# Scores stage of a graph attention kernel: engine order held to source order, outer sums placed one by one between bank reads, adjacency loads two steps ahead

## The chip, the cores and the metric

The kernel runs on one core of one Trainium2 chip. The metric is the device time of that core in microseconds, the median of several executions; lower is better. The profile is one execution taken by the hardware profiler, so its span differs slightly from the median.

A core has a matrix engine (TensorE), a vector engine (VectorE, "DVE" in the profile), an activation engine (ScalarE, "ACT"), GpSimd ("POOL") and a queue engine (SyncE, "SP"). In this kernel SyncE issues nearly all loads, and GpSimd issues the stores. The program is written with a framework that records instructions in source order, works out their dependencies, and then lets a scheduler choose the order in which each engine gets its own instructions. All data are 32-bit floats.

## What is computed

The reference has two layers on a graph of 3327 nodes with 512 features. Cut to what matters:

```python
# layer 0
h = maximum(layernorm(x), 0)
q = h @ Wq.T + bq ; k = h @ Wk.T + bk ; v = h @ Wv.T + bv
a = q @ k.T / sqrt(512) + adj + adj
x = x + softmax(a) @ v
# layer 1
h = maximum(layernorm(x), 0)
A2 = adj + eye
d = diagonal(A2) ** -0.5
temp = A2 @ h @ W.T
x = x + relu((d[:, None] * A2 * d[None, :]) @ temp)
```

The kernel multiplies large matrices in seven half-size products in place of eight (a Winograd form of Strassen's scheme), so sums and differences of blocks are formed on VectorE. The **scores stage** computes exp(2 adj + q k) for 52 steps: four groups (two strips of columns, each in two halves) of 13 row pairs. Each step multiplies a pair of row tiles of the transposed scores with 448 columns (groups 1 and 2) or 384 columns (groups 3 and 4). In the same step it forms the four block sums of A2 that layer 1 will need ("outer sums") from the adjacency blocks that are in SBUF anyway, and stores them.

## The kernel before: the parts that matter

The rings of buffers and the slots that the projection stage (the stage before) uses:

```python
    def ring(*slots):
        turn = itertools.cycle(slots)
        def take(shape, name):
            kind, k = next(turn)
            return kind(k, shape, name)
        return take

    def four_differences(b):
        nc.vector.tensor_sub(b[4], b[0], b[1])
        nc.vector.tensor_add(b[5], b[3], b[4])
        nc.vector.tensor_sub(b[6], b[1], b[3])
        nc.vector.tensor_sub(b[7], b[2], b[5])

    # ... (cut)
    x_bank, y_bank, z_bank, tp_bank = psum_ring(0, 1), psum_ring(2, 3), psum_ring(4, 5), psum_ring(6, 7)

    class Chain:                       # seven products of one step, in three PSUM banks
        before = None
        def __init__(self, product, first, more, last):
            X, Y, Z = x_bank("X"), y_bank("Y"), z_bank("Z")
            product(Y, "m1", True)
            first(0, Y, -1)
            product(Z, "p5", True)
            first(3, Z, -1)
            product(X, "p2", True)
            more(0, X)
            product(Y, "p6", False)
            first(1, Y, -1)
            Chain.finish()             # the last product of the step before
            product(Z, "p3", False)
            more(1, Z)
            product(Y, "p7", False)
            more(3, Y)
            def rest():
                product(Y, "p4", False)
                first(2, Y, 1)
                last()
            Chain.before = rest
        # ... finish() calls Chain.before (cut)

    x_ring = ring(*((mid, k) for k in range(4)))
    v_ring = ring(*((mid, k) for k in range(5, 13)))
```

The scores stage:

```python
    groups = [(s, q) for s in range(2) for q in range(2)]
    g_rings = ring(*((mid, k) for k in range(4))), ring(*((mid, k) for k in range(4, 9)))
    o_ring = ring(*((mid, k) for k in range(9, 13)))
    # ... queries(n) loads four query blocks of group n (cut)

    def more_queries(n, qt):
        # ... (cut)
        four_differences(qt)
        nc.scalar.mul(qt[0], qt[0], -1.0)

    def adjacency(s, q, t):                                  # two loads of a step
        wd, c = Q[s], q * Q[s]
        g = [take([P, 2, Q[0]], f"g{k}")[:, :, :wd] for k, take in enumerate(g_rings)]
        for k in range(2):
            # ... (cut)
            nc.sync.dma_start(g[k], src[:, :, c : c + wd])   # L416
        return g

    def outer_sums(s, q, t, g):
        wd, c = Q[s], q * Q[s]
        pair = [o_ring([P, 2, Q[0]], "o")[:, :, :wd] for _ in range(2)]
        o = [pair[m // 2][:, m % 2] for m in range(4)]
        nc.vector.tensor_add(o[0], g[0][:, 0], g[0][:, 1])   # L423
        nc.vector.tensor_add(o[1], g[1][:, 1], g[0][:, 1])
        nc.vector.tensor_add(o[2], o[1], g[0][:, 0])
        nc.vector.tensor_add(o[3], o[2], g[1][:, 0])
        for n, parts in enumerate(((0, 2, 3), (0, 1, 2, 3), (3,), (1, 2, 3))):
            k, y = divmod(n, 2)
            d = diagonal(o[0], (k * HALF + t) * P, STRIPS[s] * P + y * H[s] + c)
            for m in parts if d else ():
                nc.vector.tensor_add(o[m][:, d[0]], o[m][:, d[0]], d[1])      # L431, + identity
        for m in range(2):
            nc.gpsimd.dma_start(sumd[s][t][:, 2 * m : 2 * m + 2, c : c + wd], pair[m])   # L433

    def scores(s, q, t, qt, g):
        # ... (cut)
        def product(ps, name, start):
            for k in range(2):
                nc.tensor.matmul(ps[:, :wd], h_of(t, name, k), qt[B[name]][:, k], ...)   # L441

        def settle(k):
            # ... (cut)
            nc.scalar.activation(g[k], g[k], AF.Exp)                                     # L448
            nc.gpsimd.dma_start(pd[s][t][:, 2 * k : 2 * k + 2, c : c + wd], g[k])        # L449

        def first(n, ps, sign):                                                          # L452
            nc.vector.scalar_tensor_tensor(a[n], a[n], 2.0, ps[:, :wd], op0=ALU.mult,
                                           op1=ALU.add if sign > 0 else ALU.subtract)

        def more(n, ps):
            nc.vector.tensor_add(a[n], a[n], ps[:, :wd])                                 # L456
            if n == 1:
                settle(0)

        Chain(product, first, more, lambda: settle(1))

    steps = [(n, t) for n in range(len(groups)) for t in range(HALF)]
    coming = queries(0)
    more_queries(0, coming)
    ahead = [adjacency(*groups[n], t) for n, t in steps[:1]]
    for k, (n, t) in enumerate(steps):
        if t == 0:
            qt = coming
        if k + 1 < len(steps):
            ahead.append(adjacency(*groups[steps[k + 1][0]], steps[k + 1][1]))
        g = ahead.pop(0)
        outer_sums(*groups[n], t, g)
        scores(*groups[n], t, qt, g)
        if n + 1 < len(groups):
            if t == 4:
                coming = queries(n + 1)
            if t == 8:
                more_queries(n + 1, coming)
    Chain.finish()
```

A 32-bit matmul of the source becomes two in the trace, so one product (two source matmuls) is four matmuls there, and a step has 28.

Of the kernel before, what the change touches and what calls it, by code (L numbers as in the profile page):

```python
# [3 lines left out]

# [40 lines left out]
def graph_layers_kernel(  # L45
# [27 lines left out]
    nc = tc.nc  # L73
# [28 lines left out]
    def half(k, shape, name):  # L102
        return arena.tile(shape, F32, name=name, tag=f"half{k}")
# [7 lines left out]
# [7 lines that stand above are left out]

        return take

    const = ctx.enter_context(tc.tile_pool(name="const", bufs=1))
    dram = ctx.enter_context(tc.tile_pool(name="dram", bufs=1, space=bass.MemoryType.DRAM))
    small = ctx.enter_context(tc.tile_pool(name="small", bufs=4))
# [24 lines left out]
    sumd = [[dram.tile([P, len(SUMS), H[s]], F32, name=f"sum{s}_{t}") for t in range(HALF)] for s in range(2)]  # L148
# [9 lines left out]

    def four_differences(b):

        nc.vector.tensor_sub(b[4], b[0], b[1])
        nc.vector.tensor_add(b[5], b[3], b[4])
        nc.vector.tensor_sub(b[6], b[1], b[3])  # L163
        nc.vector.tensor_sub(b[7], b[2], b[5])

    def diagonal(a, r0, c0):


        lo, hi = max(r0, c0), min(r0 + P, c0 + a.shape[-1])
        return (slice(lo - c0, hi - c0), ident[:, lo - r0 : hi - r0]) if lo < hi else None  # L170
# [24 lines left out]
    def h_of(t, product, c):  # L195

        k = next(k for k, (a, n) in enumerate(PACKS) if a <= t < a + n)
        o = (t - PACKS[k][0]) * P
        return hp[k][:, A[product], c, o : o + P]
# [7 lines left out]
    class Chain:  # L207
# [5 lines left out]
        before = None  # L213
# [29 lines left out]
                Chain.before()  # L243
            Chain.before = None

    x_ring = ring(*((mid, k) for k in range(4)))
    v_ring = ring(*((mid, k) for k in range(5, 13)))

    def load_x(i, queue=nc.sync):
        xt = x_ring([P, D], "xt")  # L250
# [35 lines left out]
                             start=c == 0, stop=c == DC - 1)  # L286
    nc.vector.tensor_scalar(u, pu[:, :DC], scale, None, op0=ALU.mult)
    for b in (M, w_v):
        four_differences(b)
        nc.scalar.mul(b[0], b[0], -1.0)  # L290

    def h_transposed(k):
# [93 lines left out]
    groups = [(s, q) for s in range(2) for q in range(2)]  # L386
# [4 lines left out]
    def queries(n):  # L391

        s, q = groups[n]
        wd = Q[s]
        qt = [half(k, [P, 2, Q[0]], "qt")[:, :, :wd] for k in q_slots[n % 2][:4]]
        for k in range(2):
            for y in range(2):
                c = STRIPS[s] * P + y * H[s] + q * wd
                nc.sync.dma_start(qt[2 * k + y], qd[:, 2 * k : 2 * k + 2, c : c + wd])
        return qt  # L400

    def more_queries(n, qt):

        wd = Q[groups[n][0]]
        qt += [half(k, [P, 2, Q[0]], "qt")[:, :, :wd] for k in q_slots[n % 2][4:]]
        four_differences(qt)
        nc.scalar.mul(qt[0], qt[0], -1.0)

    def adjacency(s, q, t):

# [3 lines that stand above are left out]
            r0, c0 = (k * HALF + t) * P, STRIPS[s] * P  # L414
            src = adjT[r0 : r0 + P, c0 : c0 + 2 * H[s]].rearrange("p (y w) -> p y w", y=2)
            nc.sync.dma_start(g[k], src[:, :, c : c + wd])  # L416
        return g

    def outer_sums(s, q, t, g):
        wd, c = Q[s], q * Q[s]  # L420
        pair = [o_ring([P, 2, Q[0]], "o")[:, :, :wd] for _ in range(2)]
        o = [pair[m // 2][:, m % 2] for m in range(4)]
        nc.vector.tensor_add(o[0], g[0][:, 0], g[0][:, 1])  # L423
        nc.vector.tensor_add(o[1], g[1][:, 1], g[0][:, 1])  # L424
        nc.vector.tensor_add(o[2], o[1], g[0][:, 0])
        nc.vector.tensor_add(o[3], o[2], g[1][:, 0])
        for n, parts in enumerate(((0, 2, 3), (0, 1, 2, 3), (3,), (1, 2, 3))):
            k, y = divmod(n, 2)
            d = diagonal(o[0], (k * HALF + t) * P, STRIPS[s] * P + y * H[s] + c)
            for m in parts if d else ():  # L430
                nc.vector.tensor_add(o[m][:, d[0]], o[m][:, d[0]], d[1])  # L431
        for m in range(2):
            nc.gpsimd.dma_start(sumd[s][t][:, 2 * m : 2 * m + 2, c : c + wd], pair[m])  # L433

    def scores(s, q, t, qt, g):
        wd, c = Q[s], q * Q[s]
        a = [g[0][:, 0], g[0][:, 1], g[1][:, 0], g[1][:, 1]]

        def product(ps, name, start):
            for k in range(2):  # L440
                nc.tensor.matmul(ps[:, :wd], h_of(t, name, k), qt[B[name]][:, k], start=start and k == 0, stop=k == 1,  # L441
                                 skip_group_check=True)

        def settle(k):
            if k == 1 and t == HALF - 1:
                nc.scalar.activation(g[k], g[k], AF.Exp, bias=pad)
            else:
                nc.scalar.activation(g[k], g[k], AF.Exp)  # L448
            nc.gpsimd.dma_start(pd[s][t][:, 2 * k : 2 * k + 2, c : c + wd], g[k])  # L449

        def first(n, ps, sign):
            nc.vector.scalar_tensor_tensor(a[n], a[n], 2.0, ps[:, :wd], op0=ALU.mult,  # L452
                                           op1=ALU.add if sign > 0 else ALU.subtract)

        def more(n, ps):
            nc.vector.tensor_add(a[n], a[n], ps[:, :wd])  # L456
            if n == 1:
                settle(0)

        Chain(product, first, more, lambda: settle(1))  # L460

    steps = [(n, t) for n in range(len(groups)) for t in range(HALF)]
    coming = queries(0)
    more_queries(0, coming)
    ahead = [adjacency(*groups[n], t) for n, t in steps[:1]]
    for k, (n, t) in enumerate(steps):
        if t == 0:
            qt = coming
        if k + 1 < len(steps):
            ahead.append(adjacency(*groups[steps[k + 1][0]], steps[k + 1][1]))  # L470
        g = ahead.pop(0)
        outer_sums(*groups[n], t, g)
        scores(*groups[n], t, qt, g)
        if n + 1 < len(groups):
            if t == 4:
                coming = queries(n + 1)
            if t == 8:
                more_queries(n + 1, coming)
    Chain.finish()


    ROLE = {"p1": 0, "p6": 2, "p7": 4, "p5": 6, "p2": 7, "p3": 1, "p4": 5, "p8": 3}
# [30 lines left out]
    for s in range(2):  # L513
        for k0 in range(0, HT[s], 2):
            n = min(2, HT[s] - k0)
            units += [(s, k0, n, t) for t in range(HALF)]
    pts, fresh = {}, {}

    def fetch(k):
        if k < len(units):  # L520
            if k < HALF:
                fresh[k] = values(units[k][3])
            pts[k] = weights(*units[k])
# [50 lines left out]
    for k, (s, k0, n, t) in enumerate(units):  # L574
        fetch(k + 3)
        if k < HALF:
            four_differences(fresh.pop(k))
        pt = pts.pop(k)
        o = o_ring2([P, 4, 2 * P], "o")[:, :, : n * P]
        four_sums(o, pt)  # L580
        if t == 0:
            ps = seven()
            sums = sum_ring([P, 2, 2 * P], "sums")[:, :, : n * P]
            nc.vector.tensor_add(sums, pt[:, 0:2], pt[:, 2:4])
        else:
            nc.vector.tensor_add(sums, sums, pt[:, 0:2])  # L586
            nc.vector.tensor_add(sums, sums, pt[:, 2:4])
        for r, a, b in (
            ("p1", pt[:, 0], 0), ("p6", o[:, 2], 4), ("p7", o[:, 0], 5), ("p5", o[:, 1], 3),
            ("p2", pt[:, 2], 1), ("p3", o[:, 3], 2), ("p4", pt[:, 3], 6),  # L590
        ):
            for m in range(n):
                nc.tensor.matmul(ps[r][:, m * E : (m + 1) * E], a[:, m * P : (m + 1) * P], vr[t][:, b],  # L593
                                 start=t == 0 and m == 0, stop=t == HALF - 1, skip_group_check=True)
        if t == HALF - 1:
            attend(s, k0, n, sums, ps)
# [48 lines left out]
    parts = {}  # L645
# [50 lines left out]
    class Right:  # L696
# [31 lines left out]
        def make(self):  # L728
            own, r = self.own, self.r
            if r == "p5":  # L730
                nc.vector.tensor_sub(own, self.two[:, :, 0:E], self.two[:, :, E:D])  # L731
            if r == "p6":
                nc.vector.tensor_add(own, own, self.two[:, :, 0:E])
                nc.vector.tensor_sub(own, own, self.two[:, :, E:D])
                nc.gpsimd.dma_start(self.t2[:, 0 : 2 * self.n], self.b[:, 0 : 2 * self.n])
            if r in ("p7", "p4"):
                nc.vector.tensor_sub(own, own, self.one)
            if self.n == 2:
                four_differences([self.b[:, k] for k in range(8)])

    class Step:

# [106 lines left out]
    steps = [Step(g, r, s, t, rights[g, r, t]) for g in range(2) for r in ORDER for s in range(2) for t in every]  # L849
# [10 lines left out]
    for g in range(2):  # L860
        for n, r in enumerate(ORDER):
            for t, e in enumerate(every):
                k = number_of(g, n, 0, t)
# [427 lines left out]
```

## Time and profile before

| | |
|---|---|
| time, median of 3 runs | 2365.53 us (2365.27 to 2374.09) |
| span of the profiled execution | 2365.2 us |
| busy: TensorE / VectorE / ScalarE / GpSimd | 2256.0 / 1420.9 / 227.7 / 294.6 us |
| scores stage: first and last matmul start | 205.6 and 815.9 us |
| matmuls of the scores stage (L441) | 1456, that is 28 in each of 52 steps |
| an adjacency load, issue to landing | 4.1 us median (3.2 to 6.5) |
| a store of exponentials / of outer sums, issue to landing | 3.8 / 4.8 us (448 columns) |

How to read the lines that follow. A line of a list of waits has the engine and source line that waited, what it waited for, then the total in us, how often, and the longest. "PEld" is the weight load of TensorE, "SPq" the sequencer of the load queue. A timeline line has the start and the busy time in us, the engine, the line, the operation, output<-input, how many were merged, and in brackets the idle time of that engine just before and what ended it. A table of stretches gives the stretch and its length, then the busy time of each engine with its number of instructions, the granted TensorE clock as a share of full speed, the mean busy share of the 16 DMA engines, and GB/s. The profile models the ends of matmuls, so the spacing of their starts says more than their durations.

### The profile page before, as it was taken

The numbers are of one execution on the slowest core, as the hardware profiler recorded it, in microseconds if no ns is written. First come the engines' busy times: TensorE is split into PE (matmuls) and PEld (weight loads), VectorE is DVE, ScalarE is ACT, GpSimd is POOL, SyncE is SP. The second block draws the span as 40 slices with busy tenths as digits, with TensorE's granted clock in tenths as the row PEclk, the third lists the DMA queues.
The fourth block names the chain that finished last, engine by engine and source line by source line (L and its number), as shares of the span: only waits on it lengthen the run. The fifth ranks groups of instructions, "written<-read, shape, count | busy, mean of one in ns | idle before, by whom it ended". The sixth has DMA issues, their size and how long they took to land.

```text
span 2365.2 us, 22424 instructions
## 1 busy us (share of the span) xinstructions
PE 2256.0 (95%) x7522; PEld 1413.1 (60%) x7522; DVE 1420.9 (60%) x2935; ACT 227.7 (10%) x322; POOL 294.6 (12%) x462
## 2 busy tenths in 40 slices
PE   7999898988888899999999999999999999999996
PEld 4765444444544588888888755555555455555554
DVE  5436556555565556557556676777744456777674
ACT  4221111111111100000000000000000000000011
POOL 2323222222222101101011100000000000000001
PEclk8999999999999999999999999999999999999998
DMA  4336767766667634426346577766655567767684
GB/s 144 132 116 233 241 231 250 238 216 226 210 238 260 205 95 147 134 77 190 89 135 223 177 230 246 232 201 194 204 170 167 177 193 240 229 209 221 200 276 142
DMA packets 230412, 457.62 MB, mean 193 GB/s; under 512 B 25394, under 2 KB 135696, under 8 KB 230288
## 3 DMA queue, kind: packets, MB, share of 16 engines
q1 hardware_dynamic: 192464, 322.12, 44.1%
q0 software_dynamic: 37248, 132.93, 15.3%
q8 instruction: 61, 1.00, 0.2%
q10 hardware_dynamic: 576, 1.05, 0.1%
q14 instruction: 63, 0.52, 0.1%
HBM read 323.11 MB, written 132.90 MB: 193 GB/s over the span
## 4 chain that ended last, share of the span: by engine, by line
PE 59%; issue 28%; POOL 6%; DMA 4%; DVE 2%; ACT 0%; POOLq 0%; SPq 0%; DVEq 0%; ACTq 0%
PE p L768 27%; PE p L593 17%; PE p L827 4%; POOL sum L433 3%; PE p L760 2%; POOL p L449 2%; PE Y L352 2%; PE Y L321 2%; PE Z L352 1%; PE Z L321 1%; DMA p<-g 1%; DMA g<-in_adjT_dram 1%; PE mm L277 1%; POOL out_dram L88 1%; PE tp L301 0%
## 5 line engine op out<-in xcount | busy, mean ns | idle before, releaser
L768 PE MATMUL p<-part,b 128*128 128x448 f32 (+1 forms) x2352 | 835.4, 513 | 2.4 <-DVE b L731 1.6
L768 PEld LDWEIGHTS p<-part,b 128*128 128x128 f32 x2352 | 445.4, 190 | 374.1 <-issue 210.0
L441 PE MATMUL Y<-qt,hp 128*128 128x448 f32 (+1 forms) x832 | 330.9, 539 | 68.6 <-DVE g L452 68.3
L593 PE MATMUL p<-vr,o 128*128 128x256 f32 x1352 | 323.2, 380 | 3.4 <-DVE vr L163 2.2
L441 PEld LDWEIGHTS Y<-qt,hp 128*128 128x128 f32 x832 | 160.2, 197 | 220.9 <-DVE g L452 93.5
L593 PEld LDWEIGHTS p<-vr,o 128*128 128x128 f32 x1352 | 257.2, 190 | 40.0 <-DVE vr L163 2.6
L155 DVE TENSOR_TENSOR part<-part 128x896 f32<-128x896 f32 (+1 forms) x168 | 171.9, 1024 | 164.4 <-PE p L768 104.9
L593 PE MATMUL p<-vr,pt 128*128 128x256 f32 x1014 | 250.8, 380 | 0.0
L593 PEld LDWEIGHTS p<-vr,pt 128*128 128x128 f32 x1014 | 192.7, 191 | 26.6
L441 PE MATMUL Z<-qt,hp 128*128 128x448 f32 (+1 forms) x416 | 166.3, 523 | 0.0
L586 DVE TENSOR_TENSOR sums<-sums,pt 128x512 f32<-128x512 f32 (+1 forms) x84 | 54.8, 652 | 139.4 <-DMA pt<-p 139.4
L448 ACT ACTIVATE g<-g 128x896 f32<-128x896 f32 (+1 forms) x100 | 89.6, 896 | 467.5 <-DVE g L452 327.2
L452 DVE SCALAR_TENSOR_TENSOR g<-g,Y 128x448 f32<-128x448 f32 (+1 forms) x156 | 91.2, 585 | 64.0 <-PE Y L441 62.9
L423 DVE TENSOR_TENSOR o<-g 128x448 f32<-128x448 f32 (+1 forms) x52 | 30.8, 592 | 163.8 <-DMA g<-in_adjT_dram 159.2
L441 PEld LDWEIGHTS Z<-qt,hp 128*128 128x128 f32 x416 | 81.9, 197 | 70.0 <-issue 44.7
L449 POOL DMA_DIRECT2D p<-g x104 | 75.4, 725 | 290.1 <-ACT g L448 272.1
L433 POOL DMA_DIRECT2D sum<-o x104 | 75.4, 726 | 170.4 <-DVE o L424 123.7
L157 DVE TENSOR_TENSOR part<-part,part 128x384 f32<-128x384 f32 (+1 forms) x146 | 86.1, 590 | 8.9 <-DVE part L156 0.5
L156 DVE TENSOR_TENSOR part<-part,part 128x384 f32<-128x384 f32 (+1 forms) x146 | 86.1, 590 | 3.1
L760 PE MATMUL p<-part,b 128*128 128x448 f32 (+1 forms) x224 | 82.8, 513 | 0.0
L441 PE MATMUL X<-qt,hp 128*128 128x448 f32 (+1 forms) x208 | 81.1, 513 | 0.0
L566 POOL DMA_DIRECT2D x1d<-xt x26 | 14.5, 558 | 456.2 <-DVE xt L565 445.8
(174 smaller groups left out, 1924.0 us busy)
## 6 DMA issues: line engine op xcount, KB each, us to landing
part<-sum SPq DMA_DIRECT2D x104, 448.0 KB, 4.7
pt<-p SPq DMA_DIRECT2D x78, 512.0 KB, 4.1
part<-sum SPq DMA_DIRECT2D x104, 384.0 KB, 3.5
part<-in_adjT_dram SPq DMA_DIRECT2D x78, 448.0 KB, 4.3
part<-in_adjT_dram SPq DMA_DIRECT2D x78, 384.0 KB, 3.6
g<-in_adjT_dram SPq DMA_DIRECT2D x52, 448.0 KB, 4.2
sum<-o POOLq DMA_DIRECT2D x52, 448.0 KB, 4.8
p<-g POOLq DMA_DIRECT2D x52, 448.0 KB, 3.8
```

The lines of the kernel that those rows point to most:

```text
L155: nc.vector.tensor_add(o[:, 0:2], g[:, 0:4:3], g[:, 1:2].to_broadcast([P, 2, g.shape[-1]]))
L156: nc.vector.tensor_add(o[:, 2], o[:, 1], g[:, 0])
L157: nc.vector.tensor_add(o[:, 3], o[:, 2], g[:, 2])
L433: nc.gpsimd.dma_start(sumd[s][t][:, 2 * m : 2 * m + 2, c : c + wd], pair[m])
L441: nc.tensor.matmul(ps[:, :wd], h_of(t, name, k), qt[B[name]][:, k], start=start and k == 0, stop=k == 1, skip_group_check=True)
L448: nc.scalar.activation(g[k], g[k], AF.Exp)
L449: nc.gpsimd.dma_start(pd[s][t][:, 2 * k : 2 * k + 2, c : c + wd], g[k])
L452: nc.vector.scalar_tensor_tensor(a[n], a[n], 2.0, ps[:, :wd], op0=ALU.mult, op1=ALU.add if sign > 0 else ALU.subtract)
L593: nc.tensor.matmul(ps[r][:, m * E : (m + 1) * E], a[:, m * P : (m + 1) * P], vr[t][:, b], start=t == 0 and m == 0, stop=t == HALF - 1, ski ...
L760: nc.tensor.matmul(ps[("p2", "p3", "p4", "p8")[k]][:, :w], b[:, z], a[:, 0, y], start=k == 3, stop=True)
L768: nc.tensor.matmul(ps[r][:, :w], b[:, i], m, start=self.t == 0, stop=self.t == PAIRS - 1 and r in ("p1", "p5", "p6", "p7"))
L827: nc.tensor.matmul(ps, cts[s][y][d][:, k * P : (k + 1) * P], w1[d], start=d == 0, stop=d == DC - 1)
```

## The change

Three things are done, all for the scores stage. A context manager `in_order` adds a dependency without a semaphore from each instruction of VectorE, TensorE, GpSimd and SyncE in the stage's loop to the one before it on the same engine, so that the scheduler must keep the source's order among them (ScalarE is left free, and so are instructions of other stages). The outer sums become a generator: the sums for step k+1 are given out one by one, each after a bank read of step k; the pieces on the diagonal follow in twos, and the query differences of the next group one in a step. Adjacency is loaded two steps ahead in the source where it was one. With this the slots of the projection stage's x and V buffers are changed, so that the first adjacency blocks and sums find their slots free earlier. The computation is the same.

```diff
+    @contextmanager
+    def in_order(*engines):
+        traced = nc.cur_bb.bb.instructions
+        before = traced[-1]
+        yield
+        begin = next(k for k in reversed(range(len(traced))) if traced[k] is before) + 1
+        last = {}
+        for ins in traced[begin:]:
+            if ins.engine in engines:
+                if ins.engine in last:
+                    tc.add_manual_dep(ins, last[ins.engine].name, ...NoSync...)
+                last[ins.engine] = ins
@@ four_differences: each of the four operations is now yielded
-        nc.vector.tensor_sub(b[4], b[0], b[1])
+        yield nc.vector.tensor_sub(b[4], b[0], b[1])
 ... (cut: the other three likewise; other stages run the generator to its end at once)
-    x_ring = ring(*((mid, k) for k in range(4)))
-    v_ring = ring(*((mid, k) for k in range(5, 13)))
+    x_ring = ring(*((mid, k) for k in (0, 1, 2, 5)))
+    v_ring = ring(*((mid, k) for k in (9, 10, 11, 12, 3, 6, 7, 8)))
@@ more_queries
-        four_differences(qt)
+        for _ in four_differences(qt):
+            yield
         nc.scalar.mul(qt[0], qt[0], -1.0)
+        yield
@@ outer_sums
-        nc.vector.tensor_add(o[0], g[0][:, 0], g[0][:, 1])
-        nc.vector.tensor_add(o[1], g[1][:, 1], g[0][:, 1])
-        nc.vector.tensor_add(o[2], o[1], g[0][:, 0])
-        nc.vector.tensor_add(o[3], o[2], g[1][:, 0])
+        of = ((g[0][:, 0], g[0][:, 1]), (g[1][:, 1], g[0][:, 1]), (o[1], g[0][:, 0]), (o[2], g[1][:, 0]))
+        crossing = []
 ... (cut: the diagonal's marks are collected in crossing)
+        for m in range(4):
+            nc.vector.tensor_add(o[m], *of[m])
+            yield
+            if m % 2 and not crossing:
+                nc.gpsimd.dma_start(sumd[s][t][:, m - 1 : m + 1, c : c + wd], pair[m // 2])
+        for k, (m, d) in enumerate(sorted(crossing, key=lambda mark: mark[0])):
+            nc.vector.tensor_add(o[m][:, d[0]], o[m][:, d[0]], d[1])
+            if k % 2:
+                yield
-        for m in range(2):
+        for m in range(2) if crossing else ():
             nc.gpsimd.dma_start(sumd[s][t][:, 2 * m : 2 * m + 2, c : c + wd], pair[m])
@@ scores: first(...) and more(...) end with
+            next(beside, None)
@@ the loop
-    more_queries(0, coming)
-    ahead = [adjacency(*groups[n], t) for n, t in steps[:1]]
-    for k, (n, t) in enumerate(steps):
 ... (cut)
+    for _ in more_queries(0, coming):
+        pass
+    ahead = [adjacency(*groups[n], t) for n, t in steps[:2]]
+    for _ in outer_sums(*groups[0], 0, ahead[0]):
+        pass
+    with in_order(*(e.engine for e in (nc.vector, nc.tensor, nc.gpsimd, nc.sync))):
+        for k, (n, t) in enumerate(steps):
+            if t == 0:
+                qt = coming
+            g = ahead.pop(0)
+            if k + 2 < len(steps):
+                ahead.append(adjacency(*groups[steps[k + 2][0]], steps[k + 2][1]))
+            pieces_of = []
+            if k + 1 < len(steps):
+                pieces_of.append(outer_sums(*groups[steps[k + 1][0]], steps[k + 1][1], ahead[0]))
+            if n + 1 < len(groups):
+                if t == 2:
+                    coming = queries(n + 1)
+                    pieces_more = more_queries(n + 1, coming)
+                if t >= 6:
+                    pieces_of.append(itertools.islice(pieces_more, 1))
+            beside = itertools.chain(*pieces_of)
+            scores(*groups[n], t, qt, g)
+            for _ in beside:
+                pass
+        Chain.finish()
```

More of the change, by code (lines that the diff above doesn't have):

```diff
@@ L2 @@
 import math
-from contextlib import ExitStack
+from contextlib import ExitStack, contextmanager
 import concourse.bass as bass
@@ L119, in ring @@
         return take
+    @contextmanager
[8 more added lines that the diff above has]
+                if ins.engine in last:
+                    tc.add_manual_dep(ins, last[ins.engine].name,
+                                      mybir.DependencyInfo(mybir.DependencyClass.NoSync, mybir.DependencyReason.DATA),
+                                      reason="in_order")
+                last[ins.engine] = ins
     const = ctx.enter_context(tc.tile_pool(name="const", bufs=1))
@@ L159, in four_differences @@
     def four_differences(b):
-        nc.vector.tensor_sub(b[4], b[0], b[1])
-        nc.vector.tensor_add(b[5], b[3], b[4])
-        nc.vector.tensor_sub(b[6], b[1], b[3])
-        nc.vector.tensor_sub(b[7], b[2], b[5])
+        yield nc.vector.tensor_sub(b[4], b[0], b[1])
+        yield nc.vector.tensor_add(b[5], b[3], b[4])
+        yield nc.vector.tensor_sub(b[6], b[1], b[3])
+        yield nc.vector.tensor_sub(b[7], b[2], b[5])
     def diagonal(a, r0, c0):
@@ L288, in graph_layers_kernel @@
     for b in (M, w_v):
-        four_differences(b)
+        for _ in four_differences(b):
+            pass
         nc.scalar.mul(b[0], b[0], -1.0)
@@ L429, in outer_sums @@
             d = diagonal(o[0], (k * HALF + t) * P, STRIPS[s] * P + y * H[s] + c)
-            for m in parts if d else ():
-                nc.vector.tensor_add(o[m][:, d[0]], o[m][:, d[0]], d[1])
-        for m in range(2):
+            crossing += [(m, d) for m in parts] if d else []
+        for m in range(4):
[8 more added lines that the diff above has]
+        for m in range(2) if crossing else ():
             nc.gpsimd.dma_start(sumd[s][t][:, 2 * m : 2 * m + 2, c : c + wd], pair[m])
@@ L458, in more @@
                 settle(0)
+            next(beside, None)
         Chain(product, first, more, lambda: settle(1))
@@ L463, in graph_layers_kernel @@
     coming = queries(0)
-    more_queries(0, coming)
-    ahead = [adjacency(*groups[n], t) for n, t in steps[:1]]
-    for k, (n, t) in enumerate(steps):
[L467 to L479, printed above, removed]
+    for _ in more_queries(0, coming):
[22 more added lines that the diff above has]
+            for _ in beside:
+                pass
+        Chain.finish()
     ROLE = {"p1": 0, "p6": 2, "p7": 4, "p5": 6, "p2": 7, "p3": 1, "p4": 5, "p8": 3}
@@ L576, in graph_layers_kernel @@
         if k < HALF:
-            four_differences(fresh.pop(k))
+            for _ in four_differences(fresh.pop(k)):
+                pass
         pt = pts.pop(k)
@@ L738, in make @@
             if self.n == 2:
-                four_differences([self.b[:, k] for k in range(8)])
+                for _ in four_differences([self.b[:, k] for k in range(8)]):
+                    pass
     class Step:
```

## Prediction

> **What bounds the kernel now.** I read the page's busy shares and its 40 slices first. TensorE is busy 95% of the span, so only a stage in which it is not busy can give time back. The slices show full TensorE from about 850 us on; earlier, the scores stage (matmuls of line 441) has 8s and 9s. The listing of line 441 puts its first matmul at 205.6 us and its last at 815.9 us. A table of two stretches inside this stage and one of the attention stage shows the difference:
>
> ```profile
> core 0: us, PE busy (x) PEld busy (x) DVE busy (x) ACT busy (x) POOL busy (x), PEclk, DMA share, GB/s
> 233.00:505.00 272.00, 246.01 (x628) 119.81 (x629) 154.75 (x304) 43.68 (x46) 66.68 (x92) 0.98 0.69 235
> 530.00:780.00 250.00, 221.55 (x636) 125.27 (x635) 137.82 (x287) 38.11 (x45) 65.91 (x91) 0.94 0.69 232
> 900.00:1200.00 300.00, 299.61 (x1401) 263.56 (x1401) 182.39 (x450) 16.78 (x22) 30.55 (x54) 1.00 0.44 137
> ```
>
> In the scores stage no engine is full: TensorE 90% and 89%, VectorE 57% and 55%, DMA 69%. The granted clock is also below 1, while full load in attention runs at 1.00. So waits bind here, not work. The list of waits between 205 and 816 us names them:
>
> ```profile
> DVE o L423 <- DMA g<-in_adjT_dram: 159.2, 46, 6.0
> PEld Y L441 <- DVE g L452: 93.5, 47, 5.0
> PE Y L441 <- DVE g L452: 68.3, 39, 4.4
> ...
> SPq L416 <- DMA p<-g: 479.6, 95, 14.1
> ```
>
> TensorE waits for VectorE's read of a Y bank (L452). But VectorE idles itself, 159.2 us in 46 of 52 steps, always ahead of L423, the first outer sum of A2, and for an adjacency load. The load queue (last line, from the waits of the queue itself) in turn waits 479.6 us for stores of exponentials. The timeline of VectorE and TensorE from 612 us shows one turn:
>
> ```profile
> 612.20 0.56 DVE L452 SCALAR_TENSOR_TENSOR g<-g,Y 128x384 f32<-128x384 f32 x1 [0.74 <-PE Y L441]
> 617.28 0.56 DVE L423 TENSOR_TENSOR o<-g 128x384 f32<-128x384 f32 x1 [4.53 <-DMA g<-in_adjT_dram]
> 617.75 0.55 DVE L452 SCALAR_TENSOR_TENSOR g<-g,Y 128x384 f32<-128x384 f32 x1
> ...
> 610.70 2.74 PE L441 MATMUL Y<-qt,hp 128*128 128x384 f32 x8
> 613.28 1.45 PE L441 MATMUL Z<-qt,hp 128*128 128x384 f32 x4
> 614.57 1.45 PE L441 MATMUL Y<-qt,hp 128*128 128x384 f32 x4
> 618.36 1.56 PE L441 MATMUL Y<-qt,hp 128*128 128x384 f32 x4 [2.33 <-DVE g L452]
> ```
>
> The bank read at 617.75 needed only matmuls that were issued by 613.28, yet it stands behind the sum at 617.28, and that behind its load. TensorE's next product waits for it. Which step's sum is it? By 617.3 us L423 has run 37 times, while L456 on Z, once a step, has run 33 times. So the scheduled order has sums about three steps ahead of the products, whose own step number 34 is under way. Its load can only go out when the four-deep g ring gives a buffer back:
>
> ```profile
> 608.83 3.25 DMA p<-g
> 612.08 0.02 SPq L416
> 612.10 0.03 issue
> 612.13 5.05 DMA g<-in_adjT_dram
> ```
>
> That (the chain of waits in this window) closes a loop: store of one step's exponentials 608.83, landing 612.08, load landing 617.18, sum 617.28, bank read 617.75, then exponentials and the next step's store at about 620.5. One turn is 11.7 us, and that is the step's period: (816.4-205.6)/52 = 11.75 us. It is the same for the wide steps (448 columns) and the narrow ones (384), although their matmul work differs. So a latency loop, not an engine, sets the stage.
>
> **What the skill says.** "PSUM — Partial Sum Buffer", section "Engine vs sequencer instructions", says the VectorE queue is strict first in, first out; the read at 617.75 stuck behind a sum it doesn't need agrees. "TensorE: Matmul & The Clock Gate", Part 1, says an idle window of about 3.4 us drops the array's clock to half until it has been busy as long again. The trace agrees: after a 3.91 us wait that ends at 588.17 us the granted clock reads 0.70 and 0.62 in two stretches of 5 us, and eight matmuls took 5.49 us in place of 2.74. "DMA: Bandwidth & Descriptors", section "Issuing engines are not separate DMA queues", says loads and stores issued from different engines share the same 16 DMA engines; so stores and loads must be added against one limit, which I do below. No page bears on how the order is chosen.
>
> **The change part by part.**
> *Kept order, and sums one step ahead.* Work is the same: no matmul, sum or transfer is added or removed. What changes is where a sum stands: at step k only step k+1's four sums, one after each bank read. A sum costs 0.47 us (start to start) at 384 columns and 0.53 at 448. A bank is rewritten two products after it is filled at the earliest (Y: m1, p5, p2, p6): 2 x 1.29 = 2.58 us narrow, 2 x 1.505 = 3.01 us wide. A bank read begins about 0.2 us after its product and takes 0.56, plus one sum in front: 0.2+0.47+0.56 = 1.23 us, under 2.58. So one sum between reads is hidden. VectorE per narrow step: 11 operations x 0.47 = 5.2 us and one or two diagonal pieces of 0.29, some 5.7 of 9.03; wide 11 x 0.53 = 5.9 of 10.54. A query difference (0.95 to 1.09 us) comes once in a step, late, with about 1.5 us to spare.
>
> *Loads two steps ahead.* With ring depths four and five, the load for k+2 takes the buffer of step k-2 (or k-3). In a wide step the Z read that completes the first g tile comes after six products, about 9.2 us in, the exponential ends near 10.8, the store is issued at 11.1 and lands after 3.9, at 15; the load lands 4.2 later, at 19.2 us after step k-2 began. It is first used by a sum at the start of step k+1, 31.6 us after. Spare 12 us. The loop is cut: it would have to grow by a whole step to bind.
>
> *Ring slots.* V tiles take mid 3, 6 to 12, and x tiles 0, 1, 2, 5. The first two adjacency pairs (slots 0, 4 and 1, 5) and the first sums (9, 10) no longer stand on the last V stores; the third pair's slot 6 still does. I count about 2 us less front loss than now.
>
> *The sum.* Products start every 1.505 us (wide: 239.23 to 242.24 is two) and 1.29 us (narrow: 610.70 to 613.28 is two) when nothing waits. Seven a step: 10.54 and 9.03 us. 26 x 10.54 + 26 x 9.03 = 508.8 us at full clock. The stage now takes 816.4 - 205.6 = 610.8 us, about 4 of it V and attention matmuls in between. So 98 us are waits and cold clock. I expect most to go, and keep 14: 3 at the front, 4 at diagonal steps and group changes, 7 at the end, where VectorE also waits on V blocks for attention (3.3 us ahead of one at 792.15) and where step 52 drains. Saving 84 us: 2365.5 - 84 = 2281 us. Stages after it keep TensorE full and stay.
>
> **Rivals.**
> *DMA becomes the bound.* A wide step moves six 448 KB transfers, 2.75 MB; in 10.54 us that is 261 GB/s, and six of 384 KB in 9.03 us is the same. Scaling the measured traffic, 233 x 11.75 / 9.79 = 280 GB/s, share 0.69 x 1.2 = 0.83. For it: a burst of 0.98 share already appears. Against: later stages ran 331 and 350 GB/s in two stretches of 20 us (from 1340 and 1460 us), and 12 us of spare absorbs slower transfers. If it bound at share 0.75, the stage would take 611 x 0.69/0.75 = 562 us and the kernel about 2315.
> *Strict order brings waits of its own.* A sum whose load is late, a diagonal step with seven pieces, or stores kept in order on GpSimd now stop everything behind. GpSimd's four issues of 0.73 us are 2.9 a step. If each step lost 1 us: 2281 + 52 = 2333, within 2%.
> *A loop of VectorE and TensorE.* If each bank read came late by semaphore delay, products would run at less than back to back. Against: 610.70 to 614.57 ran at 1.29 with the same reads. A loss of 0.1 us on seven reads would be 36 us: 2317.
> *The next stage takes it back.* Its start is already loose (TensorE 27.8 of 30 us from 820 to 850). If V blocks or exponentials were late, perhaps 10 us: 2291.
>
> **Range and chances.** Perfect packing gives 2365.5 - 98 = 2267, and a slightly better front 2263. Half-way DMA trouble or half a microsecond a step gives about 2305. Eight in ten: 2263 to 2307. A gain of under 2% (above 2318) needs a rival to take over half of the saving: 0.07; slower by 2% needs a new stall of 2.5 us in each step, for which nothing speaks: 0.02.
>
> **What would show it.** After: the scores stage near 525 us long; the wait of L423's successor for adjacency loads near zero (from 159); TensorE over 97% busy at clock 0.99 or more; step periods near 10.5 and 9.0 that differ between wide and narrow; DMA share 0.8 or more; the load queue still waits on stores, harmlessly. I am wrong if VectorE still waits on loads, if narrow and wide steps keep one period, or if TensorE's gaps reappear behind another releaser.

## The result, and the profile after

The changed kernel takes 2266.65 us (median of 4, 2264.21 to 2269.33) where the kernel before takes 2365.4: a ratio of 0.9575, 95% interval 0.955 to 0.9601, so 98.75 us less. Measured once more, beside three of the experiments below, it took 2270.09 us against 2365.19, ratio 0.9604 (0.9589 to 0.9619).

Lines have moved: L423 and its like are now L450 (outer sums), L441 is L467 (products), L452 is L478 and L456 is L483 (bank reads), L416 is L435 (adjacency loads). The table of stretches of the changed kernel, two stretches in the scores stage, with the columns as before:

```profile
core 0: us, PE busy (x) PEld busy (x) DVE busy (x) ACT busy (x) POOL busy (x), PEclk, DMA share, GB/s
233.00:450.00 217.00, 217.00 (x579) 109.92 (x578) 147.59 (x272) 40.67 (x43) 60.88 (x84) 1.00 0.81 280
480.00:690.00 210.00, 210.00 (x652) 123.87 (x651) 147.04 (x293) 39.91 (x47) 66.69 (x92) 1.00 0.85 291
```

TensorE is busy all the time at the full granted clock, where it was 90% and 89% busy at 0.98 and 0.94. VectorE works 68% and 70% of the time, DMA runs at a share of 0.81 and 0.85. The waits of the stage, and those of the load queue:

```profile
PEld Y L467 <- DVE g L478: 6.8, 8, 2.2
PE Y L467 <- DVE g L478: 3.0, 2, 1.6
DVE o L450 <- DMA g<-in_adjT_dram: 2.7, 1, 2.7
...
SPq L435 <- DMA p<-g: 371.5, 48, 10.0
```

VectorE's 159.2 us of waiting for adjacency loads have become 2.7, TensorE's 68.3 us for bank reads 3.0. The load queue still waits 371.5 us for stores, but the sums do not wait for its loads, so this costs nothing. The timeline of one narrow step:

```profile
600.12 0.55 DVE L478 SCALAR_TENSOR_TENSOR g<-g,Y 128x384 f32<-128x384 f32 x1
600.15 1.45 PE L467 MATMUL Z<-qt,hp 128*128 128x384 f32 x4
600.58 0.55 DVE L450 TENSOR_TENSOR o<-o,g 128x384 f32<-128x384 f32 x1
601.05 0.55 DVE L478 SCALAR_TENSOR_TENSOR g<-g,Y 128x384 f32<-128x384 f32 x1
...
601.44 2.74 PE L467 MATMUL Y<-qt,hp 128*128 128x384 f32 x8
604.02 1.45 PE L467 MATMUL Z<-qt,hp 128*128 128x384 f32 x4
605.31 1.45 PE L467 MATMUL X<-qt,hp 128*128 128x384 f32 x4
```

A sum stands between two bank reads, and the products start 1.29 us apart (600.15, 601.44, two products to 604.02, 605.31) without a gap. From the first product at 202.3 us to the end of the last at 717.7 the stage lasts 515.4 us, where it lasted 610.8: 95.4 of the 102.8 us by which the two profiled spans differ. Of the rest, 3.3 us lie before the stage, but that start moves between profiles whatever the kernel (the changed kernel's is 202.3 here and 205.8 in the later one; with the old slots it is 205.6 before and 202.5 in the run with fewer buffers below); 4.1 lie after it.

The 95.4 us are not waits alone. The whole stage, before and after:

```profile
205.60:816.40 610.80, 542.23 (x1470) 284.46 (x1470) 344.48 (x697) 95.30 (x106) 153.26 (x213) 0.96 0.69 231
202.30:717.70 515.40, 512.20 (x1470) 278.93 (x1469) 352.79 (x689) 95.13 (x106) 151.77 (x211) 1.00 0.80 277
```

TensorE's idle time fell from 68.6 to 3.2 us. Its busy time for the same 1470 matmuls fell from 542.2 to 512.2 us, with a mean granted clock of 0.96 before and 1.00 after. So about 65 us are waits and 30 us faster matmuls.

### The profile page after: what moved, and what is told of

The parts are those of the page before. It is cut to its first block, busy times and chain, and to the rows that moved or that the text cites. A ratio compares the mean times of both kernels' runs of the same rounds, so it can differ in the third digit from the quotient of the medians.

```text
span 2262.4 us, 22368 instructions
## 1 busy us (share of the span) xinstructions
PE 2220.2 (98%) x7522; PEld 1405.8 (62%) x7522; DVE 1431.7 (63%) x2935; ACT 227.5 (10%) x322; POOL 294.5 (13%) x462
## 4 chain that ended last, share of the span: by engine, by line
PE 87%; issue 7%; DMA 2%; DVE 2%; POOL 1%; SPq 0%; ACT 0%; POOLq 0%; DVEq 0%; ACTq 0%
PE p L810 33%; PE p L634 18%; PE Y L467 12%; PE Z L467 6%; PE p L869 4%; PE X L467 3%; PE p L802 3%; PE Y L369 2%; PE Y L338 2%; PE Z L369 1%; PE Z L338 1%; PE mm L293 1%; POOL out_dram L88 1%; PE X L369 0%; PE tp L318 0%
## 5 line engine op out<-in xcount | busy, mean ns | idle before, releaser
L467 PE MATMUL Y<-qt,hp 128*128 128x448 f32 (+1 forms) x832 | 308.4, 513 | 3.2 <-DVE g L478 3.0
L467 PEld LDWEIGHTS Y<-qt,hp 128*128 128x128 f32 x832 | 157.8, 190 | 136.5 <-issue 73.3
L467 PE MATMUL Z<-qt,hp 128*128 128x448 f32 (+1 forms) x416 | 162.3, 513 | 0.0
L478 DVE SCALAR_TENSOR_TENSOR g<-g,Y 128x448 f32<-128x448 f32 (+1 forms) x156 | 91.6, 587 | 66.1 <-PE Y L467 64.4
L467 PEld LDWEIGHTS Z<-qt,hp 128*128 128x128 f32 x416 | 79.2, 190 | 65.9 <-issue 38.6
L467 PE MATMUL X<-qt,hp 128*128 128x448 f32 (+1 forms) x208 | 81.1, 513 | 0.0
L843 ACT COPY part<-p 128x448 f32<-128x448 f32 (+1 forms) x28 | 14.1, 505 | 588.6 <-PE p L810 558.2
L872 POOL DMA_DIRECT2D row<-ts x26 | 14.0, 539 | 435.2 <-ACT ts L871 435.2
```

## The experiments

The theory: VectorE takes its instructions in order, and the scheduler had put each outer sum so far ahead of its step that its load had to wait for the exponentials that the same VectorE queue, behind the sum, was still to complete. The rivals: that blocks of sums delay bank reads and placing them singly is what helps; that loads had too short a lead; that the order of loads and stores matters; that the stage is short of buffers.

What each order of VectorE is can be read from the compiled programs. Buffers are numbered in order of allocation; in the kernel before, a piece in the wide steps reads:

```
o<-g_2452          outer sum
o<-g_2453,g_2452   outer sum
g_2281<-g_2281,Y   bank read
o<-o,g_2452        outer sum
...
g_2323<-g_2323,Z   bank read
g_2324<-g_2324,Y   bank read
g_2363<-g_2363,Y   bank read, next step
```

Each step has a pair of g tiles, and the next pairs begin at 2323, 2363, 2412, 2452: a sum for step k+3 stands among the reads of step k. The trace has the same lead in 48 of 52 steps (counted by first sums and by reads of X, of which each step has one). The ring of first tiles is four deep, so tile 2452 takes the buffer of step k-1: its load can start only when the exponentials of step k-1 have been stored, just before the sum is due.

**Order held, sums left in blocks.** The kernel before, with the held order and the new slots alone.

```diff
+    with in_order(VectorE, TensorE, GpSimd, SyncE):
         for k, (n, t) in enumerate(steps):
             ...            # the source order of before: four sums, then the step's products
+        Chain.finish()
```

> The kernel before with one thing added: the order of VectorE, TensorE, GpSimd and the load queue is held to the source (and the new slots of x and V, without which the held order can't be scheduled). The four sums of a step still stand in one block, with their diagonal pieces, ahead of that step's own bank reads, and loads go one step ahead. Loop theory (a sum that stands about three steps ahead in VectorE's queue waits for a load that waits for the last step's store): the sum is now for the step at hand, its load is long there, so nearly all is gained, 2268 to 2290 us. Placement theory (blocks of sums delay bank reads; one by one is what helps): little gained, 2330 us or more. Lead theory (loads must go two steps ahead): 2350 us or more, VectorE waiting for adjacency loads as before.

2284.94 us, ratio 0.9678 (0.9651 to 0.9705): three quarters of the gain (3.22% of 4.25%) come with the order alone, loads one step ahead and sums in blocks. No wait of VectorE for an adjacency load is left in this stage. What it still loses is where the placement theory has its part. Its timeline behind the ninth step of the third group, where four query differences, four sums and three diagonal pieces stand in front of a read:

```profile
570.35 0.95 DVE L177 TENSOR_TENSOR qt<-qt 128x768 f32<-128x768 f32 x1
...
576.07 0.69 DVE L447 TENSOR_TENSOR o<-o,ident 128x128 f32<-128x128 f32 x3
576.68 0.55 DVE L468 SCALAR_TENSOR_TENSOR g<-g,Y 128x384 f32<-128x384 f32 x1
577.28 4.54 PE L457 MATMUL Y<-qt,hp 128*128 128x384 f32 x8 [3.57 <-DVE g L468]
```

The read comes late, TensorE waits 3.57 us, and the eight matmuls after it take 4.54 us where 2.74 is usual.

**The same, query differences spread.**

```diff
-            if t == 8:
-                more_queries(n + 1, coming)          # five operations at once
+            if t >= 6:
+                next(pieces_more, None)              # one in a step
```

> The run with order only, and one thing more: the five query operations of the next group, one in a step from the seventh on, in place of all behind the ninth step. The sums stay in blocks of four. In the run with order only, TensorE's three long waits (4.1, 2.7 and 3.6 us) stand at these blocks of query differences, each followed by matmuls at a lower clock. If they are what that run still lost: 2266 to 2274 us. If the blocks of sums and diagonal pieces are: 2280 us or more.

2280.04 us, ratio 0.9656 (0.9636 to 0.9676), between the two expectations and not told from the run without spreading by these intervals. The long waits are gone, but TensorE still waits 12.3 us for bank reads in 13 places, and its weight loads 30.5 us. The stage lasts 531.3 us here, 536.3 with order only, 515.4 in the changed kernel. These lengths don't divide the loss between sums and query differences, for spreading did not take the latter out of the way: each now stands in front of a block. One of the 13 places:

```profile
300.81 1.08 DVE L424 TENSOR_TENSOR qt<-qt 128x896 f32<-128x896 f32 x1
301.81 0.62 DVE L442 TENSOR_TENSOR o<-g 128x448 f32<-128x448 f32 x1
...
304.20 0.89 DVE L450 TENSOR_TENSOR o<-o,ident 128x128 f32<-128x128 f32 x4
305.01 0.61 DVE L471 SCALAR_TENSOR_TENSOR g<-g,Y 128x448 f32<-128x448 f32 x1
305.68 1.77 PE L460 MATMUL Y<-qt,hp 128*128 128x448 f32 x4 [0.93 <-DVE g L471]
```

In nine of the 13 (6.7 of the 12.3 us) a query difference and a block stand together before the read, as here; in the other four (5.6 us) it is instructions of the attention stage, in three of them beside a block. A block with nothing of the kind beside it, diagonal pieces or not, makes TensorE's products wait nowhere in this run. So a block is harmful only in company. That single sums are needed, once the query differences stand between reads, is not shown: no run has that alone.

**Placed, not ordered.**

```diff
-    with in_order(*(e.engine for e in (nc.vector, nc.tensor, nc.gpsimd, nc.sync))):
+    with ExitStack():
```

> The changed kernel without the held order: sums one by one between bank reads in the source, loads two ahead, new slots, but the scheduler is free. Its VectorE order has the sums of a step about three steps ahead of the products again. Loop theory: 2350 to 2375 us, VectorE again waiting 130 us or more for adjacency loads. Placement theory: 2267 to 2300 us. Lead theory: about 2267 us.

2359.39 us, ratio 0.9986 (0.9974 to 0.9998). The source has the sums singly and the loads two ahead, and the gain is gone, for the scheduler puts the sums three steps ahead again (a sum from tile 2422 stands among the reads of tiles 2295 and 2296; the pairs between begin at 2340 and 2381; in the trace it is so in 50 of 52 steps). The new slots are in this run too, so they bring nothing without the order. The list of waits of this run:

```profile
DVE o L450 <- DMA g<-in_adjT_dram: 157.0, 47, 6.2
PEld Y L467 <- DVE g L478: 87.5, 46, 4.8
PE Y L467 <- DVE g L478: 63.6, 40, 4.2
```

These are the waits of the kernel before.

**VectorE alone, and all but VectorE.**

```diff
-    with in_order(*(e.engine for e in (nc.vector, nc.tensor, nc.gpsimd, nc.sync))):
+    with in_order(nc.vector.engine):                                     # VectorE alone
+    with in_order(*(e.engine for e in (nc.tensor, nc.gpsimd, nc.sync))): # all but VectorE
```

> The changed kernel with the order held on VectorE alone; TensorE, GpSimd and the load queue are the scheduler's again. The program's order is then the same as the changed kernel's on VectorE, TensorE and ScalarE, and differs on the load queue and on GpSimd. Loop theory: VectorE's order is the whole cause, so 2262 to 2272 us. Rival, that the order of loads and stores matters too: 2285 us or more.

2267.72 us, ratio 0.9599 (0.9585 to 0.9612), beside 0.9604 for the changed kernel measured with it: all of it. Not one wait of VectorE for adjacency is left in the stage's list.

> The counterpart of the run with VectorE alone: the changed kernel with the order held on TensorE, GpSimd and the load queue, and VectorE left to the scheduler. Its VectorE order has the sums some three steps ahead again; TensorE's order is that of the changed kernel. Loop theory: the gain is gone, 2345 to 2375 us. Rival, that ordered loads and stores bring the buffers back sooner: 2300 us or less.

2346.72 us, ratio 0.9934 (0.9914 to 0.9954). Most of the gain is gone, though not quite all: VectorE waits 106.4 us for adjacency, less than the 157 with no order at all. VectorE's own order is not the same in these two runs: by the traces the first sum is three steps ahead in 31 steps here and two in 20, against three in 50 with no order at all. Whether the little that is gained comes from that or from the order of loads and stores is open. With VectorE in order, that of the others bears on nothing measurable.

**Sums three and two steps ahead, order held.** This puts the suspected cause back by hand.

```diff
-            if k + 1 < len(steps):
-                pieces_of.append(outer_sums(... steps[k + 1] ..., ahead[0]))
+            lead = min(3, max(1, k))                # or min(2, ...)
+            while loaded < min(len(steps), k + 1 + max(2, lead)):
+                ahead.append(adjacency(... steps[loaded] ...)); loaded += 1
+            while summed < min(len(steps), k + 1 + lead):
+                pieces_of.append(outer_sums(... steps[summed] ..., ahead[summed - k - 1])); summed += 1
```

> The changed kernel with its held order, but from the fourth step on the sums given out in step k are those of step k+3, and the loads go three steps ahead to serve them. Work and order of all else are the same. Loop theory: the load for step k+3 needs the buffer of step k-1, whose store ends some 4 us into step k; the sum after the first bank read stands still until its load lands, and with it all reads behind. I expect a loop of 12 to 14 us per step, 2370 to 2470 us, and VectorE waiting 150 us or more for adjacency loads. Theory that any held order with sums one by one is good: 2262 to 2275 us.

2467.7 us, ratio 1.0448 (1.0422 to 1.0474): with everything in order and every sum placed singly, the kernel is 4.5% slower than the one before. Its timeline, and its waits:

```profile
614.14 0.56 DVE L478 SCALAR_TENSOR_TENSOR g<-g,Y 128x384 f32<-128x384 f32 x1 [1.14 <-PE Y L467]
619.64 0.56 DVE L450 TENSOR_TENSOR o<-g 128x384 f32<-128x384 f32 x1 [4.94 <-DMA g<-in_adjT_dram]
620.12 0.55 DVE L478 SCALAR_TENSOR_TENSOR g<-g,Z 128x384 f32<-128x384 f32 x1
620.72 1.56 PE L467 MATMUL Z<-qt,hp 128*128 128x384 f32 x4 [1.86 <-DVE g L478]
...
DVE o L450 <- DMA g<-in_adjT_dram: 281.5, 47, 9.0
PE Z L467 <- DVE g L478: 126.3, 45, 5.9
```

The picture of before is back: a sum stands idle for its load, and a bank read that needs nothing of it stands behind. The stage lasts 717.2 us, 13.8 a step, as the loop's working had it (12 to 14). The loop is longer than in the kernel before (11.75), probably because the sum comes after the first read of a step here, so that most of the step's reads, and the exponential, follow the load; the scheduler had put the sum nearer to the exponential.

> As the run with sums three ahead, but two: the sums of step k+2 are given out in step k, loads two ahead. Loop theory: the buffer comes from step k-2, its store lands about 4.4 us into step k-1 and the load about 4.2 us later, some 1.5 to 2 us before the sum is due. So it just fits: 2266 to 2300 us, with a few waits of VectorE for loads. If lead harms in proportion: about half of the loss of three ahead, 2320 us or more.

2270.47 us, ratio 0.9616 (0.9591 to 0.9641). Two ahead just fits: five waits of VectorE for adjacency, 7.2 us together. Harm is not in proportion to the lead. It is there where ring depth less lead is one (4 - 3), and at two (4 - 2) it is nearly nothing.

**Loads one step ahead.**

```diff
-    ahead = [adjacency(*groups[n], t) for n, t in steps[:2]]
+    ahead = [adjacency(*groups[n], t) for n, t in steps[:1]]
-            if k + 2 < len(steps):
-                ahead.append(... steps[k + 2] ...)
+            if k + 1 < len(steps):
+                ahead.append(... steps[k + 1] ...)
```

> The changed kernel with the adjacency loads one step ahead in the source in place of two; the sums stay one step ahead. Loop theory: the load queue holds little else, so it runs ahead of the other engines and issues a load as soon as the ring gives the buffer of four steps before back, whatever the distance in the source: 2262 to 2272 us, as the changed kernel. Lead theory (a load issued in the step in which its sum is due comes too late): VectorE waits about 4 us a step, 2350 us or more.

2273.49 us, ratio 0.9613 (0.9597 to 0.9629), its interval overlapping that of the changed kernel beside it (0.9589 to 0.9619). The third part of the change, loads two ahead, brings nothing that these runs can measure.

**One buffer fewer in each ring of the kernel before.**

```diff
-    g_rings = ring(*((mid, k) for k in range(4))), ring(*((mid, k) for k in range(4, 9)))
+    g_rings = ring(*((mid, k) for k in range(3))), ring(*((mid, k) for k in range(4, 8)))
```

> The kernel before with one adjacency buffer fewer in each ring: three and four in place of four and five. Loop theory: the scheduler runs the sums as far ahead as the ring lets it, two steps in place of three, and the loop store, landing, load, sum, bank read, exponential, store is as long as it was, so the time stays, 2350 to 2375 us. Rival, that the kernel before is short of buffers: a tighter ring is slower, 2395 us or more.

2354.42 us, ratio 0.996 (0.9949 to 0.9971): no slower, if anything faster by 0.4%, and VectorE waits the same 157.6 us. The scheduled sums are now two steps ahead (in 50 of 52 steps of the trace) with a ring of three, again a difference of one. A ring with more buffers was not tried.

**A version that beats both.** In the changed kernel the last waits come from the stage after. V differences of attention stand between the last bank reads of scores, as this timeline of the changed kernel shows:

```profile
692.35 0.42 DVE L177 TENSOR_TENSOR vr<-vr,b 128x256 f32<-128x256 f32 x1 [3.25 <-DMA b<-vd]
692.69 0.55 DVE L478 SCALAR_TENSOR_TENSOR g<-g,Y 128x384 f32<-128x384 f32 x1
...
693.29 2.85 PE L467 MATMUL Y<-qt,hp 128*128 128x384 f32 x8 [1.39 <-DVE g L478]
```

The differences were held behind the stage's last bank read, and the blocks they need loaded into buffers that are free earlier:

```diff
-            for _ in four_differences(fresh.pop(k)):
-                pass
+            for ins in four_differences(fresh.pop(k)):
+                hold(ins)                            # ordered after the last bank read of scores
-    b12_ring = ring(*((mid, k) for k in range(4, 8)))
+    b12_ring = ring((quarter, 0), (quarter, 1), (mid, 6), (mid, 7), (mid, 8), (mid, 4))
```

> The changed kernel with the V differences of the attention stage held behind the last bank read of the scores stage, and their V blocks loaded into buffers that are free earlier. In the changed kernel some of these differences stand between the last bank reads and wait there for V blocks (3.25, 0.88, 2.15 and 0.48 us in the last three steps), and TensorE then waits 1.39 and 1.58 us; 2.5 us more are lost at the start of attention. If it is the same disease at small scale, the waits of TensorE at the end of the stage go and 2 to 5 us are gained: 2258 to 2265 us when the changed kernel has 2266. If the differences are missed at the start of attention instead, no gain: 2264 to 2272 us.

The changed kernel, once more, beside it:

> The changed kernel once more, as the measure for the three runs beside it: 2262 to 2270 us.

2259.11 us against 2270.09, ratios to the kernel before 0.9556 (0.9542 to 0.9569) and 0.9604 (0.9589 to 0.9619), which don't overlap. The stage lasts 511.2 us in place of 515.4 in the first profile of the changed kernel (516.1 in the second), and TensorE waits for no bank read in it any more. Attention, from there to its last matmul, takes 515.4 in place of 518.4 and 518.9. These are some 7 to 8 us, more than the 2 to 5 expected; the stage's part is the firmer one, for attention took 521.4 with VectorE alone in order, 3 us more than in the first profile. The medians differ by 11; about 2.4 us is the later start of scores in the profile beside it (205.8, here 203.4), which the edit doesn't explain. Holding the differences and the new buffers were not tried apart.

## Why the prediction was right

The forecast was 2281 us in a range of 2263 to 2307, with 0.91 for faster by over 2%; measured 2266.65, inside and near the low end. By its steps:

- *A loop, not an engine, sets the stage.* Shown from both sides. Holding VectorE alone takes the loop away and the whole gain appears (0.9599 beside 0.9604); putting the sums back three ahead by hand brings the waits back (281.5 us) and makes the kernel slower than before (1.0448).
- *One period for wide and narrow steps.* A wrong reading, though what it was to support holds. The prediction's own table has 628 matmuls in 272 us of wide steps and 636 in 250 of narrow ones; at 28 a step that is 12.1 and 11.0 us, and 11.75 is only the mean. Loads and stores in the loop are themselves longer in wide steps (4.2 and 3.8 us against 4.0 and 3.6). So a difference between wide and narrow steps was no sign of success, as the prediction had it. The sizes are: 10.5 and 9.0 us after (579 matmuls in 217 us, 652 in 210), as worked out.
- *The lower clock.* The prediction ties it to idle windows of about 3.4 us. The trace of before is less strict: after waits of 1.92, 2.27, 2.40, 2.53 and 2.85 us too (they end at 705.5, 477.5, 633.9, 309.4 and 375.3 us) the granted clock was 0.50 for some 3.4 us, though not after every wait of such a length. Where they differ, the measurement decides. Short waits in each step thus cost more than their own length, as the 30 us of faster matmuls show.
- *The spare of the new loads, 12 us.* Right in effect. The wide loads now take 5.5 us from issue to landing (233 to 690 us) where 4.2 was used, and the sums never wait in the steady part.
- *One sum between reads is hidden.* Right: no gap between products from 202 to 690 us. A block alone is hidden too; what costs is a block together with other work, as the run with spread differences shows.
- *508.8 us of products at full clock.* Right: with 2.6 us of V and attention matmuls in between (twelve of about 0.216 us; the prediction had 4) and 3.0 us of waits it makes 514.4; the stage took 515.4.
- *I keep 14.* This term was mis-sized, and it is most of what the forecast missed by. The front (3) and the diagonal steps and group changes (4) cost nothing visible; only the end is left, 3.0 us of waits where I put 7. In all 515.4 less 508.8 less 2.6 is 4 us kept. Another 4.1 us came after the stage, which I had left unchanged, some 2 of them in attention (520.5 us to its last matmul before, 518.4 after); no run explains them. So it is partly luck that the result lies at what the prediction called perfect packing, 2267 us.
- *Ring slots, about 2 us less front loss.* Not what they are for. In the old slots the buffers of the first sums hold the last V tiles, whose last use comes later in the held order, so that order would wait for itself; the slots make the held order possible. No run shows them by themselves.
- *Rivals.* DMA runs at the 0.83 that was worked out (0.81 and 0.85) and does not bind. Order brings no waits of its own. Nothing was taken back by the next stage.

What I had not separated was the share of each part. Order is most of it (0.9678), and VectorE's alone is enough (0.9599 beside 0.9604); placing sums and query differences singly between reads is worth 0.7 to 1% once the order is held (0.9604 and 0.9575 against 0.9678) and next to nothing without it (0.9986); the second step of lead is worth nothing measurable.

## What to carry to other kernels

When an engine with an in-order queue idles on a load, look at which step that load serves: an instruction of a later step that stands too early can lock the ring that feeds it, and then the length of that loop sets the period. The stage looks short of buffers, and need not be. Ring depth less lead is the number to watch: one stalled in all four kernels where it ruled (before, placed without order, fewer buffers, three ahead by hand), two ran almost freely. In this kernel that is shown; elsewhere it is a thing to test. Side work belongs behind the work that gives its buffers back, and holding the order of that one engine is the cheap test.

## What the runs showed that was not expected

The long waits of the run with order only stood at the query differences, yet spreading these gained nothing that the ratios show (0.9656 against 0.9678): each difference still met a block of sums. And held order is not good in itself: the same held order with the sums two steps further ahead is 9% slower (2467.7 against 2266.65 us), with a granted clock of 0.93 in the stretch from 233 to 450 us where it was 1.00. That fewer buffers did not hurt (0.996) was expected in its run, but would not be by a reader of the waits alone.
